# A gate moved from ScalarE to VectorE, and more gathered tiles for the ScalarE and SyncE queues, in a recommender's forward pass

## The chip, the cores and the metric

The kernel runs on one core of one Trainium2 chip. A core has five engines with a queue of instructions each: TensorE (PE, matrix products into PSUM), VectorE (DVE), ScalarE (ACT), GpSimd (POOL) and SyncE (SP). ACT, POOL and SP can also issue DMAs. The metric is the device time of one execution in microseconds, the median of three runs.

## The reference, cut to what matters

16384 users each have 69 ids (`batch_user`) and one label id. The table `emb` has 100001 rows of 96 floats.

```python
u = emb[batch_user]                       # 16384 x 69 x 96
ql = emb[batch_label[:, 0]]
q = jnp.broadcast_to(ql[:, None, :], u.shape)
z = jnp.concatenate([q, u, q - u, q * u], axis=-1)
h = _dice(z @ W1 + b1, a1, EPS_DICE)      # 64 sums for each id
h = h @ W2 + b2
att = h @ W3 + b3
eff = (batch_user < ITEM_NUM)[..., None]
pre = jnp.where(eff, u * att, 0.0)
pooled = jnp.einsum('gf,bfe->bge', window, pre).reshape(u.shape[0], G * E)
x = jnp.concatenate([pooled, ql], axis=-1)
# two layers with _dice (200 and 80 wide) and a last product give one number for each user

def _dice(x, alpha, eps):
    p = jax.nn.sigmoid(_bn_eval(x, eps))
    return (alpha * (1.0 - p) + p) * x
```

The gate of `_dice` is the factor `alpha * (1 - p) + p`, that is `(1 - alpha) * p + alpha`.

## The kernel before, in words

The users are cut into 32 blocks of 512. The ids of a block are cut into 69 chunks of 512 rows of the table: 64 main chunks (8 users times their first 64 fields) and 5 tail chunks (one of the last five fields for all 512 users). A step takes two chunks, so there are 1104 steps (`NPAIR`). A chunk has four tiles of 128 rows, so a step reads eight tiles of 128 rows of 96 floats.

How a tile gets into SBUF is the first thing to follow. Normally `gather` (line 265) issues one indirect DMA on POOL, which reads 128 ids and brings 128 rows into the step's buffer `u` (14 buffers in `upool`). Some chunks, called singles, have their fourth tile (`SLOT = 3`) brought in another way: row by row, as 128 DMAs of 384 bytes, from SP (109 tiles, the odd chunk of one step in ten, `SP_CHUNKS`) or from ACT (136 tiles, the even chunk of one step in eight, `ACT_CHUNKS`). These rows land in a buffer of `ring` (4 buffers for SP, 3 for ACT). The class `Singles` does this: `load` (line 283) reads 32 row offsets from SBUF into registers of the queue, and `fetch` (line 295) issues one DMA for each row at line 301. A single's gather on POOL is left out, and PE waits on a semaphore for its rows.

The order of all work is written out by hand: `plan` maps each step to its pieces, and every engine runs its own instructions in that order. In step i of the body this is: every fourth step the attention sums of four steps (`attend_rows`, ACT copies them out of PSUM at line 416); the tail's part; every fourth step their spreading (`spread`); the hidden sums of step i-2 (`hidden`); ACT's row DMAs of the step (`scalar_rows`); the pooling products of step i-7 (`pool`, `POOL_LAG`); and `fetch(i)`, which gathers, transposes on PE into `ptr` (two PSUM buffers), copies to `uT` and multiplies to `quT` on DVE. SP's tile for step m is put at step m-6, and SP's loads of ids (`load_ids`, line 151, four blocks each) 50 steps ahead of their block; SP runs on its own as soon as its ring has room. ACT's rows are 16 a step, eight steps to a tile, issued right after the gate of the same step, and they end three steps ahead of their use. A block's label rows (`head_gather`, four gathers on POOL) and its top layers (`top1` to `top3`) are spread over steps of their own; the last eight steps and what follows them are listed one by one, with the last block's top cut in quarters.

The other thing to follow is the gate. `hidden` (line 389) adds up the hidden sums of two chunks in PSUM (`ph`, two buffers). ACT then makes y = sigmoid(ph) at line 405 and y = (1 - a1) * y + a1 at line 406 (an Identity activation with a scale and a bias for each partition), and DVE multiplies y = ph * y at line 407. PE reads y in `attend_rows`, `attend_tail`.

Of the kernel before, what the change touches and what calls it, by code (L numbers as in the profile page):

```python
# [14 lines left out]
AF = mybir.ActivationFunctionType  # L15
ALU = mybir.AluOpType
PSUM = bass.MemoryType.PSUM

P = 128
# [29 lines left out]

ROW_BYTES = 4 * E  # L50
SLOT = 3
SP_CHUNKS = [2 * (10 * s + 8) + 1 for s in range(109)]
SP_RING = 4
ACT_CHUNKS = [2 * (8 * s + 11) for s in range(136)]
ACT_RING = 3
ACT_ROWS = 16
ACT_STEPS = -(-P // ACT_ROWS)
SINGLES = SP_CHUNKS + ACT_CHUNKS
NSB = (len(SINGLES) + P - 1) // P
NSEM = 8  # L60


def chunk_of(c):

    n, k = divmod(c, NCH)
    if n == NBLK - 1 and k >= EARLY:
        k = NMAIN + k - EARLY if k < EARLY + NTAIL else k - NTAIL
    return n, k
# [47 lines left out]
def rec_kernel(  # L116
# [12 lines left out]
    nc = tc.nc  # L129
# [1 line left out]

    const = ctx.enter_context(tc.tile_pool(name="const", bufs=1))
    ipool = ctx.enter_context(tc.tile_pool(name="ipool", bufs=2))
    upool = ctx.enter_context(tc.tile_pool(name="upool", bufs=14))
    tpool = ctx.enter_context(tc.tile_pool(name="tpool", bufs=4))
    ypool = ctx.enter_context(tc.tile_pool(name="ypool", bufs=6))
    rpool = ctx.enter_context(tc.tile_pool(name="rpool", bufs=2))
# [60 lines left out]
    a1c = NEAR.of(wn, "a1")  # L198
    na1c = const.tile([P, 1], F32, name="na1c")
# [75 lines left out]
    class Singles:  # L275

        def __init__(self, name, engine, kind, chunks, first, buffers, group):
            self.name, self.engine, self.kind, self.group = name, engine, kind, group
            self.chunks, self.first, self.buffers = chunks, first, buffers
            self.sems = [tc.alloc_semaphore(f"{name}{k}") for k in range(NSEM)]  # L280
            self.given = [0] * NSEM

# [12 lines left out]
        def fetch(self, s, start, stop):  # L295

            b, k = self.buffers[s % len(self.buffers)], s % NSEM
            for r in range(start, stop):
# [90 lines left out]
    def hidden(i, uT, quT):  # L389

        ph = ps_h.tile([P, 512], F32, tag="h", name=f"ph{i}")
        places = [chunk_of(2 * i + j) for j in range(2)]
        sums = [ph[j * H1 : (j + 1) * H1, :] for j in range(2)]
        for (n, k), p in zip(places, sums):
            if k >= NMAIN:
                nc.tensor.matmul(p, Cq, qTs[n % 2], start=True, stop=False)  # L396
        for j, ((n, k), p) in enumerate(zip(places, sums)):
            if k < NMAIN:
                nc.tensor.matmul(p, As[n % 2][:, k // 4, :], uT[j], start=True, stop=False)  # L399
            else:  # L400
                nc.tensor.matmul(p, A, uT[j][0:E], start=False, stop=False)  # L401
        for j, p in enumerate(sums):
            nc.tensor.matmul(p, Wp, quT[:, j, :], start=False, stop=True)  # L403
        y = ypool.tile([P, 512], F32, tag="y", name=f"y{i}")
        nc.scalar.activation(y, ph, AF.Sigmoid, scale=S_DICE)  # L405
        nc.scalar.activation(y, y, AF.Identity, bias=a1c, scale=na1c)  # L406
        nc.vector.tensor_mul(y, ph, y)  # L407
        return y

    def attend_rows(b, n):  # L410
# [156 lines left out]
    def hidden_of(k):  # L567
        return lambda: ys.__setitem__(k, hidden(k, *hs[k]))
# [25 lines left out]
    def at(step, *work):  # L594
        plan.setdefault(step, []).extend(work)

    by_sync = Singles("sp", nc.sync, mybir.EngineType.SP, SP_CHUNKS, 0, range(SP_RING), 32)
    for s, m in enumerate(SP_CHUNKS):
        at(max(0, m // 2 - 6), lambda s=s: by_sync.fetch(s, 0, P))

    by_scalar = Singles(
        "act",
        nc.scalar,
        mybir.EngineType.Activation,
        ACT_CHUNKS,
        len(SP_CHUNKS),
        range(SP_RING, SP_RING + ACT_RING),
        2 * ACT_ROWS,
    )
    turn = {}  # L610
    for s, m in enumerate(ACT_CHUNKS):
        for k in range(ACT_STEPS):
            turn.setdefault(m // 2 - 2 - ACT_STEPS + k, []).append((s, k * ACT_ROWS, min(P, (k + 1) * ACT_ROWS)))

    def scalar_rows(i):

        for s, start, stop in turn.get(i, []):
            by_scalar.fetch(s, start, stop)

    c = NPAIR - CLOSE  # L620
    for i in range(c):
        if i >= 3 and (i - 3) % 4 == 3:
            at(i, rows_of(i - 6, 4))
        if i >= 3:
            at(i, tails_of(i - 3))
        if i >= 4 and (i - 4) % 4 == 3:
            at(i, spread_of(i - 7, 4))
        if i >= 2:
            at(i, hidden_of(i - 2))
        at(i, lambda i=i: scalar_rows(i))  # L630
        if i < c - CLOSE:
            if i >= POOL_LAG:
                at(i, pool_of(i - POOL_LAG))
        else:

            for k in {0: (-15, -14), 1: (-13,), 3: (-12, -11), 4: (-10, -9), 7: (-8, -7)}.get(i - c + 8, ()):
                at(i, pool_of(c + k))
        at(i, fetch_of(i))
# [116 lines left out]
```

## Time and profile before

| | |
|---|---|
| median of 3 runs | 10925.68 us (10925.35 to 10929.42) |
| profiled execution | 10926.71 us, span 10924.9 us |
| PE busy | 8862.0 us, 81% |
| POOL busy | 8226.3 us, 75%, 8715 gathers |
| DVE busy | 4285.5 us, 39% |
| ACT busy | 1897.5 us, 17%, beside 17408 row DMAs |
| SP | 13952 row DMAs |
| mean granted TensorE clock | 0.745 of full speed |

In the profile an engine's share is its busy time over the span. Issuing a DMA from ACT or SP, reading registers and waiting are not counted as busy, so ACT's 17% leaves out its row DMAs; a `q` after an engine's name (ACTq, SPq) marks such instructions of its queue. A group's row has the line, engine, operation, what is written and read and how often; after the bar its busy time and the mean ns of one; after the second bar the engine's idle time just before, and what ended it. "issue" as a releaser means that the profile shows nothing the engine waited for.

### The profile page before, as it was taken

The numbers are of one execution on the slowest core, as the hardware profiler recorded it, in microseconds if no ns is written. First come the engines' busy times: TensorE is split into PE (matmuls) and PEld (weight loads), VectorE is DVE, ScalarE is ACT, GpSimd is POOL, SyncE is SP. The second block draws the span as 40 slices with busy tenths as digits, with TensorE's granted clock in tenths as the row PEclk, the third lists the DMA queues.
The fourth block names the chain that finished last, engine by engine and source line by source line (L and its number), as shares of the span: only waits on it lengthen the run. The fifth ranks groups of instructions, "written<-read, shape, count | busy, mean of one in ns | idle before, by whom it ended". The sixth has DMA issues, their size and how long they took to land.

```text
span 10924.9 us, 172203 instructions
## 1 busy us (share of the span) xinstructions
PE 8862.0 (81%) x41797; PEld 4319.5 (40%) x41797; DVE 4285.5 (39%) x7535; ACT 1897.5 (17%) x2761; POOL 8226.3 (75%) x8721
## 2 busy tenths in 40 slices
PE   7878878788887888888878778878888887888878
PEld 3333434343333344333433333334343333433335
DVE  4334333333333333433333333333333333333334
ACT  1111111111111111111111111111111111111112
POOL 7777777777777777777777777777777777777776
PEclk7767777777777777767777777777777777777777
DMA  2212211121111212212111121112212112122111
GB/s 49 42 42 44 42 42 41 42 44 42 42 42 42 44 41 42 42 41 44 42 42 41 42 44 42 42 42 42 44 42 42 42 41 44 42 42 41 42 41 36
DMA packets 344467, 458.51 MB, mean 42 GB/s; under 512 B 202354, under 2 KB 202866, under 8 KB 343330
## 3 DMA queue, kind: packets, MB, share of 16 engines
q0 software_dynamic: 278880, 428.92, 18.7%
q1 hardware_dynamic: 29762, 11.82, 0.5%
q10 hardware_dynamic: 34816, 6.75, 0.4%
q8 instruction: 336, 5.51, 0.2%
q14 instruction: 673, 5.51, 0.2%
HBM read 446.74 MB, written 0.07 MB: 41 GB/s over the span
## 4 chain that ended last, share of the span: by engine, by line
POOL 49%; issue 21%; PE 17%; DMA 12%; DVE 0%; ACT 0%; ACTq 0%; POOLq 0%; DVEq 0%
POOL u L266 48%; DMA u<-in_rows,ids 12%; PE p L502 4%; PE acc L325 4%; PE ph L399 3%; PE ph L403 2%; PE ptr L325 2%; POOL q L266 1%; PE prow L414 1%; PE pa L423 1%; PE ph L396 0%; PE ph L401 0%; PE pc L348 0%; PE patt L431 0%; ACTq L301 0%
## 5 line engine op out<-in xcount | busy, mean ns | idle before, releaser
L266 POOL DMA_INDIRECT u<-in_rows,ids x8587 | 8104.3, 944 | 2620.1 <-issue 2428.2
L325 PE MATMUL ptr<-ident,u 128*96 128x128 f32 x8587 | 2002.8, 332 | 1940.1 <-DMA u<-in_rows,ids 1892.9
L407 DVE TENSOR_TENSOR y<-ph,y 128x512 f32<-128x512 f32 x1104 | 763.5, 692 | 4377.1 <-ACT y L406 4119.6
L325 PEld LDWEIGHTS ptr<-ident,u 128*96 128x96 f32 x8587 | 1139.7, 149 | 2701.4 <-DMA u<-in_rows,ids 2262.6
L325 PEld LDWEIGHTS acc<-rw,u 128*96 128x96 f32 x15930 | 1677.0, 187 | 1204.3 <-issue 977.6
L376 DVE COPY uT<-ptr 96x512 f32<-96x512 f32 x2208 | 1494.1, 677 | 1488.6 <-PE ptr L325 1485.2
L325 PE MATMUL acc<-rw,u 128*96 128x20 f32 x15930 | 1792.5, 258 | 57.8 <-DVE rw L436 41.7
L405 ACT ACTIVATE y<-ph 128x512 f32<-128x512 f32 x1104 | 658.6, 597 | 6308.6 <-PE ph L403 5822.7
L399 PE MATMUL ph<-uT,A 128*64 128x512 f32 x4096 | 1649.8, 883 | 0.0
L403 PE MATMUL ph<-quT,wn 96*64 96x512 f32 x4416 | 1585.2, 788 | 0.0
L379 DVE TENSOR_TENSOR quT<-ptr,qT 96x512 f32<-96x512 f32 x2048 | 1380.2, 674 | 0.0
L406 ACT ACTIVATE y<-y,wn,na1c 128x512 f32<-128x512 f32 x1104 | 898.1, 813 | 36.6
L403 PEld LDWEIGHTS ph<-quT,wn 96*64 96x64 f32 x4416 | 440.7, 188 | 1041.5 <-issue 1040.8
L502 PE MATMUL p<-pooled,wf 96*100 96x512 f32 (+1 forms) x1400 | 693.1, 644 | 0.0
L399 PEld LDWEIGHTS ph<-uT,A 128*64 128x64 f32 x4096 | 264.1, 175 | 616.2 <-issue 608.8
L416 ACT COPY row<-prow 128x512 f32<-128x512 f32 (+1 forms) x277 | 161.6, 583 | 1791.9 <-PE prow L414 1179.1
L470 DVE COPY pooled<-acc 96x160 f32<-96x160 f32 x1008 | 419.9, 417 | 117.6 <-PE acc L325 116.9
L414 PE MATMUL prow<-y,v 128*32 128x512 f32 x2208 | 453.6, 891 | 1.4 <-DVE y L407 1.1
L502 PE MATMUL p<-pre,V 96*100 96x512 f32 (+1 forms) x700 | 394.9, 710 | 3.0 <-DVE x L485 2.7
L502 PEld LDWEIGHTS p<-pooled,wf 96*100 96x100 f32 x1400 | 259.5, 198 | 332.6 <-issue 332.6
L436 DVE SCALAR_TENSOR_TENSOR rw<-patt,bb,wn 128x320 f32<-128x320 f32 x554 | 276.2, 539 | 143.6 <-PE patt L431 142.9
L431 PE MATMUL patt<-ident,row 128*128 128x128 f32 x1108 | 224.9, 340 | 25.1 <-DVE pre L424 22.7
(72 smaller groups left out, 2445.8 us busy)
## 6 DMA issues: line engine op xcount, KB each, us to landing
ring<-in_rows ACTq DMA_DIRECT2D x17408, 0.4 KB
ring<-in_rows SPq DMA_DIRECT2D x13952, 0.4 KB
u<-in_rows,ids POOLq DMA_INDIRECT x8587
ids<-in_idx SPq DMA_DIRECT2D x8, 560.0 KB, 3.9
q<-in_emb,ids POOLq DMA_INDIRECT x128
wf<-in_far SPq DMA_DIRECT2D x1, 1209.0 KB, 6.4
wn<-in_near SPq DMA_DIRECT2D x1, 236.0 KB, 2.8
ids<-in_idx SPq DMA_DIRECT2D x1, 140.0 KB, 2.3
```

The lines of the kernel that those rows point to most:

```text
L266: nc.gpsimd.indirect_dma_start(out=dst, out_offset=None, in_=table, in_offset=bass.IndirectOffsetOnAxis(ap=index, axis=0),)
L325: ins = op(out, ring[:, at[0]].bitcast(F32) if at else u[:, 4 * (c % 2) + t, :], other, **how)
L376: nc.vector.tensor_copy(uT[j][0:E], ptr)
L379: nc.vector.tensor_tensor(quT[:, j, :].rearrange("e (s f) -> e s f", f=FM), ptr.rearrange("e (s f) -> e s f", f=FM), by_field(q[:, k * NS ...
L399: nc.tensor.matmul(p, As[n % 2][:, k // 4, :], uT[j], start=True, stop=False)
L403: nc.tensor.matmul(p, Wp, quT[:, j, :], start=False, stop=True)
L405: nc.scalar.activation(y, ph, AF.Sigmoid, scale=S_DICE)
L406: nc.scalar.activation(y, y, AF.Identity, bias=a1c, scale=na1c)
L407: nc.vector.tensor_mul(y, ph, y)
L414: nc.tensor.matmul(pr[32 * k : 32 * (k + 1), :], v2, ys[b + k], start=True, stop=True)
L470: nc.vector.tensor_copy(pooled[n][:, :, k * NS : (k + 2) * NS].rearrange("e g s -> e s g"), pa.rearrange("e j s g -> e (j s) g"),)
L502: nc.tensor.matmul(p1, w[:, h * DH : (h + 1) * DH], x, start=(k == 0), stop=(k == KTOP - 1))
```

## The change

The gate's second operation leaves ACT. With s the sigmoid, DVE makes y = (s * (1 - a1)) * ph and then y = ph * a1 + y, two scalar_tensor_tensor operations in place of one product. ACT is left with the sigmoid. More tiles become singles: SP has 199, one every 5.5 steps, with a ring of 8 buffers; ACT has 187, with a ring of 4, and its rows are one stream of 22 a step, in order, whatever tile they belong to, ending two steps ahead of the tile's use. `u` has a fifteenth buffer. The space in SBUF for the descriptors of POOL's DMAs, 16384 bytes of each partition by default, is set to 4096.

```diff
-SP_CHUNKS = [2 * (10 * s + 8) + 1 for s in range(109)]
-SP_RING = 4
-ACT_CHUNKS = [2 * (8 * s + 11) for s in range(136)]
-ACT_RING = 3
-ACT_ROWS = 16
-ACT_STEPS = -(-P // ACT_ROWS)
+SP_CHUNKS = [2 * (int(5.5 * s) + 6) + 1 for s in range(199)]
+SP_RING = 8
+ACT_ROWS = 22
+ACT_CHUNKS = [2 * ((s + 1) * P // ACT_ROWS + 2) for s in range(187)]
+ACT_RING = 4
...
+RING_BYTES = 4096
...
-    upool = ctx.enter_context(tc.tile_pool(name="upool", bufs=14))
+    upool = ctx.enter_context(tc.tile_pool(name="upool", bufs=15))
...
         nc.scalar.activation(y, ph, AF.Sigmoid, scale=S_DICE)
-        nc.scalar.activation(y, y, AF.Identity, bias=a1c, scale=na1c)
-        nc.vector.tensor_mul(y, ph, y)
+        nc.vector.scalar_tensor_tensor(y, y, na1c, ph, ALU.mult, ALU.mult)
+        nc.vector.scalar_tensor_tensor(y, ph, a1c, y, ALU.mult, ALU.add)
...
-        2 * ACT_ROWS,
+        32,
...
-    turn = {}
-    for s, m in enumerate(ACT_CHUNKS):
-        for k in range(ACT_STEPS):
-            turn.setdefault(m // 2 - 2 - ACT_STEPS + k, []).append((s, k * ACT_ROWS, min(P, (k + 1) * ACT_ROWS)))
-
     def scalar_rows(i):
 
-        for s, start, stop in turn.get(i, []):
-            by_scalar.fetch(s, start, stop)
+        row, stop = i * ACT_ROWS, min((i + 1) * ACT_ROWS, len(ACT_CHUNKS) * P)
+        while row < stop:
+            s, start = divmod(row, P)
+            n = min(P - start, stop - row)
+            by_scalar.fetch(s, start, start + n)
+            row += n
...
-    nc = bacc.Bacc("TRN2", target_bir_lowering=False, num_devices=1)
+    nc = bacc.Bacc("TRN2", target_bir_lowering=False, num_devices=1, dynamic_dma_scratch_size=RING_BYTES)
```

## The prediction

> **What bounds the kernel now.** I read the page first, then the instructions on the tiles `u` and `ring`, then the waits, then short timelines.
>
> ```profile
> span 10924.9 us, 172203 instructions
> ...
> PE 8862.0 (81%) x41797; PEld 4319.5 (40%) x41797; DVE 4285.5 (39%) x7535; ACT 1897.5 (17%) x2761; POOL 8226.3 (75%) x8721
> ...
> L266 POOL DMA_INDIRECT u<-in_rows,ids x8587 | 8104.3, 944 | 2620.1 <-issue 2428.2
> L325 PE MATMUL ptr<-ident,u 128*96 128x128 f32 x8587 | 2002.8, 332 | 1940.1 <-DMA u<-in_rows,ids 1892.9
> ```
>
> By busy share PE looks like the limit. But POOL's idle time is "issue": it waits for nothing the profile shows, 0.30 us after each 0.944 us gather, while PE's idle time before its transposes (ptr) is a wait for those gathers. The chain of work says the same: POOL 49%, issue 21%, DMA 12%, PE 17%.
>
> ```profile
> L266 POOL DMA_INDIRECT u<-in_rows,ids x8587: 940/944/1092, 8.8 to 10886.8; - x200
> ```
>
> ```profile
> L266 POOL DMA_INDIRECT q<-in_emb,ids x128: 940/944/1334, 3.3 to 10418.6; - x128
> ```
>
> 8587 + 128 = 8715 gathers start from 3.3 to 10886.8 us: 10883.5/8714 = 1.249 us each, with no gap over 0.3 us (waits). POOL is a metronome from start to end; 3.3 us lie before it and 10924.9 - 10886.8 = 38.1 us after its last start. So time is the number of gathers x 1.249 us plus about 41 us, as long as everybody else keeps up.
>
> The others' room: transposes start on average 5.3 us after their gather's start (trace, paired one by one), at most 26 us, and with 14 buffers of u, each freed seven steps later, POOL would stall only at some 60 us. The two row streams (shortest, median and longest ns of an instruction):
>
> ```profile
> L301 ACTq DMA_DIRECT2D ring<-in_rows x17408: 213/213/530, 18.4 to 10748.1; - x198
> L301 SPq DMA_DIRECT2D ring<-in_rows x13952: 227/228/463, 6.3 to 10459.8; - x200
> ```
>
> The offset loads that go with them, and SP's own waits:
>
> ```profile
> L286 ACTq TENSOR_LOAD <-offsets x544: 2132/2182/2236, 16.1 to 10735.1; - x182
> L286 SPq TENSOR_LOAD <-offsets x436: 2027/2174/2411, 4.1 to 10447.1; - x146
> ```
>
> ```profile
> SPq L301 <- PE ptr L325: 3556.9, 71, 95.2
> SPq L301 <- PE acc L325: 1324.8, 26, 96.8
> ```
>
> SP waits 4882 us for free ring buffers: it is idle nearly half the time. On ACT a row of 384 bytes, its register move included, costs what the spacing in a timeline shows:
>
> ```profile
> 5000.03 9.90 SPq L301 DMA_DIRECT2D ring<-in_rows  x31
> ```
>
> ```profile
> 5007.62 0.81 ACT L406 ACTIVATE y<-y,wn,na1c 128x512 f32<-128x512 f32 x1
> 5007.68 4.77 ACTq L301 DMA_DIRECT2D ring<-in_rows  x16
> ```
>
> (9.90 - 0.23)/30 = 0.322 us per row on SP, (4.77 - 0.21)/15 = 0.304 on ACT; over all adjacent starts under 0.6 us apart the means are 0.3255 and 0.320, and ACT's is 0.326 while SP also issues. ACT's sequencer goes on to the rows as soon as the Identity has started.
>
> [...] ACT's 213 ns become 223 to 241 ns beside SP's stream. [...] The trace shows the first reader 2.4 us after a gather's start, so two or three gathers are in flight.
>
> **The change part by part.**
>
> 1. Singles: 109 + 136 = 245 tiles become 199 + 187 = 386. POOL loses 141 gathers of 8715: 141 x 1.249 = -176.1 us. The step falls from 8715 x 1.249/1104 = 9.86 us to 8574 x 1.249/1104 = 9.70.
>
> 2. SP: 199 tiles, each 128 x 0.3255 + 4 offset loads of 2.18 (2.25 with the moves around them) = 41.7 + 9.0 = 50.7 us, against 5.5 steps x 9.70 = 53.4 us. Hidden with 5% to spare; the ring of 8 lets it run tiles ahead (a buffer is asked for 44 steps after its predecessor was due, and released after 7 to 8). The ids loads queued behind SP's rows (0.4 us of issue each) are planned 50 steps early. If the cover goes, tile after tile comes late and PE waits.
>
> 3. ACT: per step it was 16 rows, half an offset load, sigmoid and Identity: about 16 x 0.32 + 0.5 x 2.25 + 0.63 (the Identity waits for the sigmoid) = 6.9 us. It becomes 22 x 0.326 = 7.17, 22/32 loads x 2.25 = 1.55, and about 0.3 for dispatch and for row copies and the top's activations ahead of a sigmoid: 9.0 us of 9.70. Hidden, but only by 7%. Queued behind those rows is the next sigmoid, so a late ph (PE to ACT) now meets a queue busy for up to 9.7 us (a step with a load) instead of 8.1. Waiting for it: y on DVE, behind it the copies pooled and uT/quT, and then PE's next acc and ptr. PE has most of a step before it needs them, ACT's own least cycle stays under POOL's step, and PE's own step is 8862/1104 = 8.03 us, so lags come and are made up. Cost on the path in the body: 0.
>
> 4. DVE: the product (0.692 us) becomes two scalar_tensor_tensor on 128x512. Nearest rows: the pre STT, 0.741 us, and the x STT on 100x512, 0.751, both PSUM with SBUF. 1104 x (2 x 0.75 - 0.69) = 894 us more, 5180 us or 48% of the span: hidden under POOL's cadence. Bounds 0.69 and 0.85 each give 760 and 1115 us, both hidden. ACT loses 1104 x 0.813 = 898 us. Sigmoid to y stays about 2.1 us (0.60 + 0.81 + 0.69 before, 0.60 + 2 x 0.75 after).
>
> 5. POOL's descriptor space, 16384 by default to 4096 bytes: no row shows its price. Gathers 1024 apart (568, 1592, 2616 and so on) take 961 instead of 944 ns[...]; four times as often is 34 x 17 ns = 0.6 us. From below: nothing says a smaller ring makes POOL faster. From above: if each gather had to ask for space, the price is unknown; 176.1/8574 = 20.5 ns per gather would eat the gain. I take 0.
>
> 6. The fifteenth buffer of u is one more step of room: 0. Doubled offsets (128 x 512 integers): two DVE operations of 0.29 us become about 0.6 at the start, beside POOL: 0.
>
> 7. The end is where PE nearly sets the pace, as these windows of 200, 200 and 87 us show:
>
> ```profile
> 10400.00:10600.00 200.00, 155.45 (x778) 78.69 (x780) 79.01 (x138) 34.27 (x50) 151.18 (x161) 0.71 0.20 41
> 10600.00:10800.00 200.00, 168.96 (x798) 90.10 (x795) 75.43 (x135) 37.22 (x56) 151.20 (x161) 0.79 0.19 41
> 10800.00:10887.00 87.00, 78.60 (x451) 50.77 (x449) 39.53 (x72) 18.53 (x30) 65.67 (x71) 0.76 0.19 40
> ```
>
> PE is busy 155.45/200 = 78% in the first, 84% in the second and 90% in the last. Its lag behind POOL climbs to 25 us near 10650, falls to 5 by 10730, climbs to 25 near 10760 and is 4 to 7 at the last gather. With ACT at 9.0 us a step PE can no longer run the first recovery at 7 to 8 us a step (ACT's rows last to step 1088), and two more singles lie in the last 24 steps, 2.5 us less of POOL. I estimate +8 us at the end, between 0 and 20.
>
> Sum against the profiled execution, 10926.71 us: -176.1 + 8 = 10758.6. It stands 1.0 us over the median of the three runs, 10925.68; so 10758 us, -1.5%.
>
> **The rivals.**
>
> A, partial: ACT and PE don't overlap ideally at 93% load. In steps where PE itself takes 10 to 11.6 us (the qT and A rows, the top's matmuls) ACT starves, and afterwards it makes up 0.7 us a step at most. For: that small margin, and the jitter of ph (5 to 14 us between successive sums, nine times in ten). Against: taking the longer of PE's own time and 9.0 us step by step gives 9.2 to 9.3 us, still under 9.70. If it averages 9.8: +0.1 x 1088 = +109 us, 10,867.
>
> B, slower: ACT's sequencer becomes the bound. One stream tied to the sigmoids can't run ahead. Its threshold is 9.70 us a step to begin to show, (10926 - 45 - 157)/1088 = 9.86 us to lose everything (157 us: the last 16 steps). At a row cost of 0.37 us beside a busier SP: 8.14 + 1.55 + 0.3 = 10.0, hence 1088 x 10.0 + 157 + 45 = 11,080 us.[...] Against: ACT's 7555 adjacent rows beside SP already average 0.326.
>
> C, the small descriptor space stalls POOL: at +30 ns a gather, 10758 + 257 = 11,015.[...]
>
> D, SP falls behind: over 53.4 us a tile it bounds; at 55, 199 x 55 + 9 x 9.9 + 45 = 11,080. Against: 50.7, and ACT beside it moves SP's row only from 0.325 to 0.326.
>
> **How the numbers follow.** Forecast 0.76 (10,748 to 10,780); A 0.13 (10,780 to 10,904); B 0.06, C 0.03 and D 0.02 mostly slower. A measurement of this kernel can tell about 0.2%, 22 us, from no change. Most of A is faster, its edge the same; B, C and D give slower 0.10. Faster 0.87, same 0.03, slower 0.10. The floor is 8574 x 1.249 + 41 = 10,750, less a little for the unsure end: low 10,745. High 10,840 takes in the nearer half of A and leaves out under 2 in 10.
>
> **What would show it.** POOL: 8446 gathers of u at 1.249 us, idle only "issue". PE still waits for u, less than 1893 us. ACT's idle time before the sigmoid shrinks, with waits on "issue" larger than 117 us. SP's waits for the ring fall from 4882 to about 500 us. Two STT groups of 0.75 us. Wrong if POOL shows waits over 0.3 us, if a gather's period has changed, if PE's waits move from u to ring (late rows) or to DVE, or if the tail after POOL's last gather exceeds 60 us.

## The result, and the profile after

| | before | after |
|---|---|---|
| median | 10926.22 us (10924.22 to 10931.77) | 10939.76 us (10930.91 to 10947.42) |
| profiled execution, its span | 10926.71, 10924.9 us | 10932.42, 10930.6 us |
| gathers on POOL | 8715 | 8574 |
| mean of start to start | 1.249 us | 1.270 us |
| after POOL's last gather has started | 38.1 us | 43.1 us |

The ratio is 1.0012, with an interval of 95% from 1.0005 to 1.0019: the kernel is not 168 us faster, as forecast, but slower by 0.12%, which is less than the 0.2% that the prediction held to be the least that can be told from no change. These are the lines of the page of the kernel after that answer to those shown of before, with its queues and the shares of its chain.

```profile
span 10930.6 us, 207736 instructions
...
PE 8797.1 (80%) x41797; PEld 4332.6 (40%) x41797; DVE 5119.1 (47%) x8639; ACT 985.9 (9%) x1657; POOL 8093.3 (74%) x8580
...
q0 software_dynamic: 274368, 421.98, 20.3%
q1 hardware_dynamic: 52802, 16.42, 2.6%
q10 hardware_dynamic: 47872, 9.29, 2.1%
...
POOL 31%; DMA 29%; issue 15%; PE 14%; ACTq 9%; DVE 1%; ACT 1%; POOLq 0%
...
L266 POOL DMA_INDIRECT u<-in_rows,ids x8446 | 7971.7, 944 | 2752.6 <-issue 2321.2
L325 PE MATMUL ptr<-ident,u 128*96 128x128 f32 x8446 | 1893.5, 331 | 1604.8 <-DMA u<-in_rows,ids 1536.7
L406 DVE SCALAR_TENSOR_TENSOR y<-y,na1c,ph 128x512 f32<-128x512 f32 x1104 | 824.5, 747 | 4201.6 <-ACT y L405 4137.7
...
L407 DVE SCALAR_TENSOR_TENSOR y<-ph,wn,y 128x512 f32<-128x512 f32 x1104 | 829.3, 751 | 39.0
```

The 141 gathers are gone and a gather still takes 944 ns. But POOL's idle time before a gather has risen from 2620.1 us for 8587 (0.305 us each) to 2752.6 us for 8446 (0.326 us each). From start to start a gather takes 0.0206 us more (1.2696 for 1.2490): 0.0206 us x 8573 intervals = 177 us, and the gathers saved were worth 176.1 us. With 5.0 us more after the last gather, that accounts for the profiled execution: 10924.9 - 176.1 + 177 + 5.0 = 10930.8 against a span of 10930.6 us. In the chain, DMA has gone from 12% to 29%.

Which wait it is, the waits of POOL say (idle us in total, times, longest). Before:

```profile
POOL u L266 <- issue: 2428.2, 7958, 0.3
...
POOL u L266 <- DMA u<-in_rows,ids: 111.1, 364, 0.3
```

After:

```profile
POOL u L266 <- issue: 2321.2, 7552, 1.5
...
POOL u L266 <- DMA u<-in_rows,ids: 314.1, 632, 2.5
```

Before, no wait is longer than 0.3 us whatever it is put down to, so these are only labels on the ordinary pause between two gathers. After, POOL waits up to 2.5 us, and the releaser is a DMA that writes `u`: an earlier gather of its own. A timeline of POOL in a bad stretch shows one such knot (start, duration, and in brackets the idle time just before and its releaser):

```profile
3750.46 0.94 POOL L266 DMA_INDIRECT u<-in_rows,ids  x1 [0.30 <-issue]
3752.01 0.94 POOL L266 DMA_INDIRECT u<-in_rows,ids  x1 [0.61 <-DMA u<-in_rows,ids]
3753.82 0.94 POOL L266 DMA_INDIRECT u<-in_rows,ids  x1 [0.87 <-DMA u<-in_rows,ids]
3755.69 0.94 POOL L266 DMA_INDIRECT u<-in_rows,ids  x1 [0.92 <-DMA u<-in_rows,ids]
```

Which gather it waits for is in the trace's semaphore events. In this program a gather adds 1 to its semaphore sixteen times (all sixteen stand in the trace for 8044 of the 8574 gathers after, some are missing for the others), and the semaphores of the gathers are eight, 122 to 129, in rotation. A gather starts once the one eight back has all its sixteen: of 8036 such pairs none starts less than 0.258 us after the sixteenth. For the gather at 3753.82 us, the one eight back had started 10.85 us earlier; fifteen of its increments had come by 2.42 us after its start, the sixteenth at 10.59 us. POOL went on 0.26 us later. Over all gathers whose sixteen increments are in the trace:

```
from a gather's start, us                 before    after
15th increment, median                      2.46     2.49
16th increment, median                      2.52     7.60
16th increment, 95% of gathers are below    3.63    10.14
a row DMA, from its issue to its last byte, median   0.9    4.3 to 4.4
a row's data packet, median ns              22       173 to 175
```

Fifteen sixteenths of each gather land as fast as before. One sixteenth is late, and so are the rows. Eight gathers at 1.249 us are 9.99 us; less the 0.26 us, a sixteenth that lands more than some 9.7 us after its gather's start should stop POOL (an estimate), and that is the upper end of the distribution after. Of the 8036 pairs, 386 have a gather that starts over 0.1 us late, and in 322 of these the sixteenth had taken more than 9.7 us.

What the one late share has in common with the rows is, in my reading, their place: one of the sixteen DMA engines that the page counts. The packets speak for it. A row DMA has one data packet of 384 bytes and one packet of 4 bytes, by size and number its increment (ACT's queue q10 holds 2 x 17408 packets before and 2 x 23936 after), where a gather has sixteen data packets of 3072 bytes and sixteen of 4 (q0: 32 x 8715 = 278880 before). The trace doesn't number its DMA engines, so that all rows lie on the same one isn't seen; that exactly one share of sixteen is late fits it. The queues' shares say how much the rows' part is. Of before:

```profile
q0 software_dynamic: 278880, 428.92, 18.7%
q1 hardware_dynamic: 29762, 11.82, 0.5%
q10 hardware_dynamic: 34816, 6.75, 0.4%
```

The last column is a share of sixteen engines. 0.9% for the two rows' queues (q1 SP, q10 ACT) would be at most 14% of one engine, if all rows lie there (SP's queue also carries the ids and weights, 0.2%); after, 2.6 + 2.1 = 4.7% would be at most 75% of one, on top of that engine's part of the gathers, some 20% if their sixteen shares are alike. Packets' times overlap (those of the two queues add up to 8198 us after and cover 6472), so this is a sign and not an occupancy: the rows have grown by a factor of 1.58 (49408 for 31360), the two queues' time by 5.

The stalls are not spread evenly. Windows of the kernel after (busy us and number of instructions of PE, PEld, DVE, ACT and POOL, then clock, DMA share and GB/s):

```profile
1000.00:2000.00 1000.00, 799.50 (x3712) 389.66 (x3714) 460.43 (x773) 88.04 (x147) 726.96 (x771) 0.74 0.26 42
2000.00:3000.00 1000.00, 805.83 (x3763) 386.88 (x3755) 459.81 (x768) 88.71 (x148) 723.56 (x767) 0.74 0.26 41
4500.00:5500.00 1000.00, 799.15 (x3842) 394.06 (x3838) 467.80 (x788) 89.84 (x151) 747.78 (x793) 0.75 0.26 43
6000.00:7000.00 1000.00, 807.67 (x3871) 401.23 (x3872) 473.44 (x797) 89.79 (x152) 751.34 (x797) 0.75 0.26 43
```

The same window before:

```profile
2000.00:3000.00 1000.00, 805.04 (x3841) 387.99 (x3839) 388.21 (x682) 174.97 (x254) 755.66 (x801) 0.75 0.20 42
```

POOL starts 767 gathers in the third thousand microseconds against 801 before, later 793 to 797. Up to about 3800 us SP runs ahead: it has waited for free buffers of the ring 2.5 us in all until 3500 us, and issues 2.50 rows per us, which is all it can (128 rows in 50.7 us are 2.52). ACT adds 2.17, together 4.67 rows per us with 0.770 gathers. Then SP's eight buffers are full, its rate falls to 2.38, and together the two make 4.64 rows per us with 0.795 gathers. The sixteenth increment has its median at 9.0 us in the first stretch (1000 to 3500 us) and at 6.9 us in the second (4000 to 10000 us). Before, it was 1.28 + 1.62 = 2.9 rows per us.

### The profile page after: what moved, and what is told of

The parts are those of the page before. It is cut to its first block, busy times and chain, and to the rows that moved or that the text cites. A ratio compares the mean times of both kernels' runs of the same rounds, so it can differ in the third digit from the quotient of the medians.

```text
span 10930.6 us, 207736 instructions
## 1 busy us (share of the span) xinstructions
PE 8797.1 (80%) x41797; PEld 4332.6 (40%) x41797; DVE 5119.1 (47%) x8639; ACT 985.9 (9%) x1657; POOL 8093.3 (74%) x8580
## 4 chain that ended last, share of the span: by engine, by line
POOL 31%; DMA 29%; issue 15%; PE 14%; ACTq 9%; DVE 1%; ACT 1%; POOLq 0%
POOL u L266 31%; DMA u<-in_rows,ids 28%; ACTq L301 7%; PE p L502 3%; PE acc L325 2%; ACTq L286 2%; PE ph L403 2%; PE ph L399 2%; PE ptr L325 2%; PE prow L414 1%; PE pa L423 1%; PE ph L396 0%; PE ph L401 0%; POOL q L266 0%; DMA q<-in_emb,ids 0%
## 5 line engine op out<-in xcount | busy, mean ns | idle before, releaser
L266 POOL DMA_INDIRECT u<-in_rows,ids x8446 | 7971.7, 944 | 2752.6 <-issue 2321.2
L325 PE MATMUL ptr<-ident,u 128*96 128x128 f32 x8446 | 1893.5, 331 | 1604.8 <-DMA u<-in_rows,ids 1536.7
L406 DVE SCALAR_TENSOR_TENSOR y<-y,na1c,ph 128x512 f32<-128x512 f32 x1104 | 824.5, 747 | 4201.6 <-ACT y L405 4137.7
L399 PE MATMUL ph<-uT,A 128*64 128x512 f32 x4096 | 1606.4, 860 | 0.0
L403 PE MATMUL ph<-quT,wn 96*64 96x512 f32 x4416 | 1553.4, 773 | 0.0
L407 DVE SCALAR_TENSOR_TENSOR y<-ph,wn,y 128x512 f32<-128x512 f32 x1104 | 829.3, 751 | 39.0
L502 PE MATMUL p<-pooled,wf 96*100 96x512 f32 (+1 forms) x1400 | 634.7, 598 | 0.0
L414 PE MATMUL prow<-y,v 128*32 128x512 f32 x2208 | 528.0, 884 | 90.2 <-DVE y L407 85.1
L502 PE MATMUL p<-pre,V 96*100 96x512 f32 (+1 forms) x700 | 427.8, 761 | 23.6 <-DVE x L485 23.3
L485 DVE SCALAR_TENSOR_TENSOR x<-p,wf,g 100x512 f32<-100x512 f32 (+3 forms) x105 | 73.9, 704 | 508.6 <-ACT g L484 508.6
```

What stands on the lines that cost most here:

```text
L266: nc.gpsimd.indirect_dma_start(out=dst, out_offset=None, in_=table, in_offset=bass.IndirectOffsetOnAxis(ap=index, axis=0),)
L325: ins = op(out, ring[:, at[0]].bitcast(F32) if at else u[:, 4 * (c % 2) + t, :], other, **how)
L406: nc.vector.scalar_tensor_tensor(y, y, na1c, ph, ALU.mult, ALU.mult)
L407: nc.vector.scalar_tensor_tensor(y, ph, a1c, y, ALU.mult, ALU.add)
L414: nc.tensor.matmul(pr[32 * k : 32 * (k + 1), :], v2, ys[b + k], start=True, stop=True)
L502: nc.tensor.matmul(p1, w[:, h * DH : (h + 1) * DH], x, start=(k == 0), stop=(k == KTOP - 1))
```

## The experiments

**Theory** (E in the texts below). All rows queue at one DMA engine. Up to some rate they cost a gather nothing; near that engine's limit the gather's share there waits behind rows, and past eight gathers of delay POOL stalls. It must vanish with fewer rows, whichever queue they leave from, and shrink if SP can't run ahead. **Rivals** after the result: the smaller descriptor space slows POOL (R; rival C of the prediction); the gate's second operation holds up DVE's other work, and with it PE, or disturbs POOL (G); ACT's queue with its 22 rows a step sets the pace (S); SP's stream alone, or ACT's alone, is at fault. And, within the theory, two readings of "limit": so many bytes, or so many DMAs.

**The two edits that had been priced at nothing, each alone on the kernel before.** First the descriptor space:

```diff
-num_devices=1)
+num_devices=1, dynamic_dma_scratch_size=4096)
```

> The kernel before with POOL's descriptor space cut from 16384 to 4096 bytes, and nothing else. Theory E (the row DMAs of SP and ACT fill one of the 16 DMA engines, so that engine's share of each gather lands late and POOL waits for the gather eight back): no change, 10,926 us within 10, last share of a gather landing 2.5 us after its start. Rival R (the small descriptor space delays the gathers or stalls POOL): slower, 10,926 + about 176 us = 11,100, since in the changed kernel the stalls add up to 172 us over nearly as many gathers.

Measured: 10927.34 us beside 10927.04 of the kernel before, ratio 1.0000 (0.9991 to 1.0009). The sixteenth increment comes at 2.53 us. Then the gate:

```diff
-nc.scalar.activation(y, y, AF.Identity, bias=a1c, scale=na1c)
-nc.vector.tensor_mul(y, ph, y)
+nc.vector.scalar_tensor_tensor(y, y, na1c, ph, ALU.mult, ALU.mult)
+nc.vector.scalar_tensor_tensor(y, ph, a1c, y, ALU.mult, ALU.add)
```

> The kernel before with the gate on VectorE alone (two scalar_tensor_tensor for the Identity and the product), rows and rings as before. Theories E, R and S (ScalarE's 22 rows a step, at about 9 us of its queue, set the pace): no change, 10,926 us within 10. Rival G (the two longer operations on VectorE hold up uT and pooled, and with them PE): slower, 10,935 or more.

Measured: 10928.14 us, ratio 1.0000 (0.9991 to 1.0009), sixteenth increment at 2.53 us. Rivals R and G are out; both costs of nothing were right.

**SP's singles back to 109, all else as in the kernel after.**

```diff
-SP_CHUNKS = [2 * (int(5.5 * s) + 6) + 1 for s in range(199)]
-SP_RING = 8
+SP_CHUNKS = [2 * (10 * s + 8) + 1 for s in range(109)]
+SP_RING = 4
```

> The changed kernel with SP's old tiles, 109 at one in ten steps with a ring of 4; ScalarE keeps its 22 rows a step and 187 tiles, the descriptor space stays at 4096. 296 singles leave 8960 - 296 = 8664 gathers. Theory E: SP's half load frees the DMA engine, POOL runs at 1.249 us again: 8664 x 1.249 + 41 = 10,862 us, to 10,875 with some loss at the end; last landing back at 2.5 to 4 us. Rivals S and R: ScalarE's queue and the descriptor space are as they were, so still 10,930 to 10,945.

Measured: 10863.14 us beside 10927.04, ratio 0.9941 (0.9924 to 0.9958). With 296 singles 8664 gathers are left, and 8664 x 1.249 + 41 = 10,862. The waits of POOL in this kernel:

```profile
POOL u L266 <- issue: 2422.3, 7938, 0.3
POOL u L266 <- DMA u<-in_rows,ids: 89.1, 292, 0.3
```

Nothing is longer than 0.3 us again, at 3.52 rows per us. ACT's stream of 22 rows a step is therefore not the fault by itself, and S is out; every gather saved pays.

**Only SP's ring back from 8 to 4 buffers.** All rows and all 8574 gathers stay.

```diff
-SP_RING = 8
+SP_RING = 4
```

> The changed kernel with SP's ring cut from 8 to 4 buffers; the same 386 singles and the same instructions otherwise. Theory E: SP can run ahead by about 1.6 tiles instead of 5.6, so its stretch at full speed (2.50 rows per us, up to 3800 us in the changed kernel, gathers 1.30 us apart) ends after some 1000 us; then 2.38 rows per us and 1.257 us per gather. That saves (1.30 - 1.257) x about 2200 gathers = 95 us: 10,845 us, between 10,815 and 10,870. Rivals S and R: no change, 10,940; a rival of late rows (SP has too little lead) would make it slower, over 10,950.

Measured: 10859.06 us (10842.96 to 10870.47), ratio 0.9941 (0.9924 to 0.9957). Its windows:

```profile
1000.00:2000.00 1000.00, 805.45 (x3815) 397.40 (x3816) 467.96 (x788) 90.15 (x152) 743.16 (x789) 0.75 0.26 42
2000.00:3000.00 1000.00, 810.32 (x3888) 393.31 (x3890) 473.23 (x797) 91.49 (x153) 751.40 (x797) 0.76 0.27 43
```

The stretch in which SP runs ahead ends by about 1000 us instead of 3800, and the window from 2000 to 3000 us has 797 gathers in place of 767. That fits the ring's size: four buffers are 512 rows, and SP gains on its readers by 2.50 less 128/(5.5 x 10.1) = 2.30 rows per us, so they last some 2600 us. (10.1 us is the step while POOL stalls.) Somewhat under half of the lost gain (81 of 182 us) was thus the buffers that I had counted as SP's safety. The rest stays: in the profiled execution, the fastest of the four, the median of the sixteenth is still 7.1 us, and the stalls add up to 82 us.

**ACT's singles back to 136, SP's left at 199.** The other queue, to see whether it matters whose rows go.

```diff
-ACT_ROWS = 22
-ACT_CHUNKS = [2 * ((s + 1) * P // ACT_ROWS + 2) for s in range(187)]
+ACT_ROWS = 16
+ACT_CHUNKS = [2 * ((s + 1) * P // ACT_ROWS + 2) for s in range(136)]
```

> The changed kernel with ScalarE back at 16 rows a step and 136 tiles; SP keeps 199 tiles and its ring of 8. 335 singles leave 8960 - 335 = 8625 gathers. Theory E: SP at full speed with ACT gives 2.50 + 1.62 = 4.1 rows per us, under the 4.65 at which the engine was full, so no stall even while SP runs ahead: 8625 x 1.249 + 41 = 10,814 us, to 10,825. A rival in which SP's running ahead is harmful whatever ACT does[...]: still stalls early, 10,880 or more.

Measured: 10816.19 us beside 10927.62, ratio 0.9899 (0.9879 to 0.9919); 8625 x 1.249 + 41 = 10,814. Its rows' queues:

```profile
q1 hardware_dynamic: 52802, 16.36, 0.8%
q10 hardware_dynamic: 34816, 6.75, 0.5%
```

SP's queue carries exactly the packets that it carries in the kernel after, and their share is 0.8% where it was 2.6%. POOL has no wait for a gather over 0.3 us, at 4.12 rows per us:

```profile
POOL u L266 <- DMA u<-in_rows,ids: 99.2, 325, 0.3
```

So SP's stream isn't the fault by itself either; the sum is.

**Spreading a row over the engines.** Two kernels wrote the row as 16 or as 2 pieces, in the hope that each piece would go to another engine:

```diff
-out=ring[r : r + 1, b], in_=row_bytes[:, bass.ds(self.values[r], ROW_BYTES)]
+out=ring[r : r + 1, b].rearrange("p (k n) -> p k n", k=16),
+in_=row_bytes[:, bass.ds(self.values[r], ROW_BYTES)].rearrange("p (k n) -> p k n", k=16),
```

> The changed kernel with each row DMA written as 16 pieces of 24 bytes instead of one of 384[...]. Theory E says that today the rows lie on one engine: then the gap between the 15th and the 16th share of a gather's landing (2.5 and 7.6 us) closes. If an engine's time for a row goes with its bytes, POOL returns to 1.249 us and the time to about 10,755; if each piece costs an engine nearly what the row costs, all 16 fill up and all shares land late: 10,940 or more. The issue spacing on SP and ACT may also grow with 16 pieces: over 0.35 us a row SP's tile of 5.5 steps no longer fits and the time goes over 10,940 for that reason, which the row spacing would show. Against E: a lone 16th share still landing near 7.6 us.

> The same with two pieces of 192 bytes for each row. Theory E with cost by bytes: one engine's load of rows halves, two shares of each gather land somewhat late (2.5 to 4 us) and the time is about 10,755. With cost by piece: both engines are as full as one was, two shares land at 7 to 8 us, and the time stays at 10,940.

Measured: 10942.23 and 10947.20 us, one time each. The trace shows the same single packet of 384 bytes for each row as before: pieces that follow each other in memory had been put together again. These are two repetitions of the kernel after, and say nothing of spreading. So the pieces were set apart, in a second copy of the table with gaps between a row's pieces (an input prepared with it), two of 192 bytes or sixteen of 24:

```diff
-in_=row_bytes[:, bass.ds(self.values[r], ROW_BYTES)]
+in_=row_bytes[:, bass.ds(self.values[r], 416)].rearrange("p (k n) -> p k n", k=2)[:, :, 0:192]
```

> The changed kernel, but the rows of the singles are read from a second copy of the table in which each row lies as two halves of 192 bytes, 16 bytes apart, so that a row's DMA keeps two pieces (in the two runs meant for this before, the pieces were merged back into one of 384 bytes). Theory E, rows on one engine: the pieces go to two engines. With an engine's time going by bytes its load of rows halves: the 15th and 16th share of a gather land at 2.5 to 4 us, POOL returns to 1.25 us, 10,755 to 10,800. With time by piece: two engines are as full as one was, the 15th and 16th share both land near 7.5 us, and the time stays at 10,940. Against E: only the 16th is late, as before. If the queues take over 0.35 us to issue a row of two pieces, SP falls behind and the time is over 10,940 for that reason.

> The same with 16 pieces of 24 bytes, 8 bytes apart (512 bytes a row). By bytes: every engine gets a sixteenth of the rows' load, all shares land at 2.5 to 3 us, POOL at 1.249 us, 10,750 to 10,765. By piece: all 16 shares land late, 7 us or more, 10,940 or more. Queues slower than 0.35 us a row: SP late, over 10,940, with PE waiting for ring.

Measured: 21013.61 us with two pieces (ratio 1.923, 1.917 to 1.929) and 18513.91 us with sixteen (1.694, 1.689 to 1.699). SP's instructions for the rows in the first of the two (shortest, median, longest ns):

```profile
L302 SPq DMA_DIRECT2D ring<-in_apart x25472: 2/616/1547, 6.9 to 20893.4; - x199
```

Issuing such a row takes SP 616 ns in place of 228, rows start 0.73 us apart (median), and the chain of this kernel is SP's own queue:

```profile
SPq 83%; issue 14%; ACTq 1%; PE 1%; DMA 0%; DVE 0%; ACT 0%; POOL 0%; POOLq 0%
```

The pieces did stay apart: a row has two data packets of 192 bytes and two of 4 in the one kernel, sixteen of 24 and sixteen of 4 in the other (q10: 4 x 23936 = 95744 packets and 32 x 23936 = 765952). Whether the pieces went to as many engines was not shown. The sixteenth increment is back at 2.48 us, but at 2.4 rows per us that says nothing: it is 2.52 us at the 2.90 of before. Both kernels are failures as tests of the engine. Whether rows can be spread without paying for it in the issue stays open.

**By bytes or by number.** Each row DMA moves only the first 96 of its 384 bytes; three quarters of each single's row are left out of the computation.

```diff
-out=ring[r : r + 1, b], in_=row_bytes[:, bass.ds(self.values[r], ROW_BYTES)]
+out=ring[r : r + 1, b, 0:96], in_=row_bytes[:, bass.ds(self.values[r], 96)]
```

It ran beside a version with SP's tiles 5.75 steps apart (below). There the kernel before itself took 13766.58 us where its median was 10,926 to 10,928 everywhere else, so nothing is read from this pair, and both were run again.

> The changed kernel with each row DMA moving only the first 96 of the 384 bytes; the other three quarters of a single's row stay zero, so this part of the gather is left out. Number of row DMAs, issue and waits as in the changed kernel. Theory E with an engine's time going by bytes: the load of rows falls to a quarter, the 16th share of a gather lands at 2.5 to 3 us and POOL runs at 1.249 us: 8574 x 1.249 + 41 = 10,750, to 10,765. With time going by the number of rows: nothing changes, 10,940, the 16th share at 7.6 us. In between, by both. A rival that lays the loss to anything else than what the rows move (ScalarE's queue, the gate, SP's lead): 10,940.

> Between the best run so far (SP every 6 steps, 369 singles, 10,792 us) and the changed tiles with a ring of 4 (SP every 5.5 steps, 386 singles, 10,859): SP every 5.75 steps, 190 tiles, ring of 4; 377 singles leave 8583 gathers, floor 8583 x 1.249 + 41 = 10,761. Theory E: 128/(5.75 x 9.72) + 22/9.72 = 4.55 rows per us, just under the 4.65 at which the engine was full, and SP gains only 5.2 us a tile while it fills its ring, so stalls for some 1100 us: 10,785 to 10,825. If the limit is a matter of singles and not of rates: between 10,792 and 10,859 in proportion, 10,825.

These gave 16743.60 and 16437.67 us. Again:

> The changed kernel with each row DMA moving only the first 96 of the 384 bytes (three quarters of a single's row are left out), once more, on a chip where the kernel before takes its usual 10,926 us; the first time that kernel took 13,767 us beside it. With an engine's time going by bytes: the 16th share of a gather lands at 2.5 to 3 us, POOL at 1.249 us, 10,750 to 10,765. By the number of rows: nothing changes, 10,940, 16th share at 7.6 us. A rival that lays the loss to anything else than what the rows move: 10,940.

Measured: 10923.55 us (10918.31 to 10935.37) beside 10927.60, ratio 0.9998 (0.9988 to 1.0007). The queues:

```profile
q1 hardware_dynamic: 52802, 9.09, 3.3%
q10 hardware_dynamic: 47872, 2.39, 3.2%
```

A quarter of the rows' bytes, and the packets' times add up to more, not less: 6.5% of sixteen engines would be 104% of one. Here too the times overlap (laid over each other, those of the two queues cover 5857 us of 10927). The sixteenth increment comes at 7.31 us (7.60 with whole rows). POOL's idle time before gathers is in this line of the page:

```profile
L267 POOL DMA_INDIRECT u<-in_rows,ids x8446 | 7993.7, 946 | 2723.5 <-issue 2334.1
```

It is 147 us over the 8446 x 0.305 of an undisturbed POOL (177 with whole rows). So five sixths of the stalls are still there with a quarter of the bytes. By itself this run can't tell a limit by number from a loss that has nothing to do with what the rows move; the runs with fewer rows rule the latter out. Together they say that between 96 and 384 bytes what counts is mainly the number of DMAs.

**Fewer rows, to find where the limit lies.** SP with 182 tiles, one every six steps, and four buffers, ACT as in the kernel after:

```diff
-SP_CHUNKS = [2 * (int(5.5 * s) + 6) + 1 for s in range(199)]
-SP_RING = 8
+SP_CHUNKS = [2 * (6 * s + 6) + 1 for s in range(182)]
+SP_RING = 4
```

> Meant to beat both: the changed kernel with SP at one tile in 6 steps (182 tiles) and a ring of 4. 369 singles leave 8591 gathers: floor 8591 x 1.249 + 41 = 10,771 us. Theory E: rows at 128/(6 x 9.72) + 22/9.72 = 4.46 per us in the steady part, below 4.65, so stalls only in the first 800 us while SP fills its ring: 10,775 to 10,795. If the engine is already full at 4.46, or ScalarE's queue costs something of its own: over 10,810.

Measured: 10792.06 us (10785.50 to 10792.36) beside 10927.62, ratio 0.9875 (0.9858 to 0.9891). Then 190 tiles, 5.75 steps apart:

```diff
+SP_CHUNKS = [2 * (int(5.75 * s) + 6) + 1 for s in range(190)]
+SP_RING = 4
```

> SP every 5.75 steps, 190 tiles, ring of 4, once more, for the same reason; 377 singles leave 8583 gathers, floor 8583 x 1.249 + 41 = 10,761. Theory E: 4.55 rows per us in the steady part, just under the 4.65 at which the engine was full: 10,785 to 10,825. If the loss goes with the number of singles alone: in proportion between 369 and 386, 10,825.

Measured: 10786.15 us (10783.33 to 10787.03) beside 10927.60, ratio 0.9871 (0.9854 to 0.9887). This is faster than both kernels, by 1.3% and 1.4%. Its page and its waits:

```profile
q1 hardware_dynamic: 50498, 15.91, 2.1%
q10 hardware_dynamic: 47872, 9.29, 1.7%
...
L266 POOL DMA_INDIRECT u<-in_rows,ids x8455 | 7981.6, 944 | 2596.6 <-issue 2402.3
```

```profile
POOL u L266 <- issue: 2402.3, 7866, 0.7
...
POOL u L266 <- DMA u<-in_rows,ids: 110.3, 331, 2.4
```

POOL's idle time is 2596.6/8455 = 0.307 us a gather, next to the 0.305 of before; stalls are 17 us, nearly all of them in the first 1000 us. 8583 x 1.249 + 41 = 10,761; the stalls and a tail of 43.8 us in place of 38.1 make most of the rest. The two versions, with 8591 and 8583 gathers, can't be told apart by their times. All kernels that carried whole rows and weren't bound by SP's queue, in order of their rate in steady running:

```
                              rows per us   16th increment   stalls of POOL   time
before                           2.90           2.52 us           2 us        10926.22
SP 109, ACT 187                  3.52           2.64              2           10863.14
SP 199, ACT 136                  4.12           2.79              2           10816.19
SP 182, ACT 187                  4.46           3.97              8.5         10792.06
SP 190, ACT 187                  4.55           4.97             17           10786.15
SP 199, ACT 187, ring of 4       4.64           7.11             82           10859.06
SP 199, ACT 187 (after)      4.67, 4.64         7.60            172           10939.76
```

Stalls are start to start beyond 1.249 us, where it is over 0.1 us, in the profiled execution; 2 us of them are some longer gathers in the first 130 us, in every kernel. The rates differ by up to 2% between stretches of one run. The delay is nearly flat to 4.1 rows per us, doubles by 4.55 and runs away at 4.64. With 0.8 gathers per us, that is where gathers begin to give way. It fits the two stretches of the kernel after as well: where SP pushes more rows in, fewer gathers pass (4.67 with 0.770, 4.64 with 0.795). That the losses come to just the 176 us of the gain is a coincidence of these rates, as the ring of four buffers shows.

## Why the prediction was wrong

The forecast of 10758 us and its range from 10,745 to 10,840 both missed; no change within 0.2% had been given 3 in 100. By its own steps:

1. **Singles, -176.1 us.** The count and the 944 ns were right. The error is in the factor 1.249: the view showed POOL as a metronome, and the sum took its period for a property of POOL. It is one only while the gather eight back has landed in time. Where fewer rows go beside them, the gathers left out pay in full: 51 of them with SP's 109 tiles (10863 us, 10,862 by the same formula), 90 with ACT's 136 (10816 and 10,814).
2. **SP, 50.7 of 53.4 us.** Right in its rate (2.50 rows per us seen, 2.52 worked out), wrong in its reading. "Hidden with 5% to spare; the ring of 8 lets it run tiles ahead" counted the lead as safety; it put more rows beside the gathers for 3800 us (4.67 per us, and 0.770 gathers), and taking half of the ring away gave 80 us back. SP's waits for the ring fell from 4882 to 319 us, 500 predicted:

```profile
SPq L301 <- PE ptr L325: 253.9, 76, 16.0
SPq L301 <- PE acc L325: 63.6, 11, 14.5
```

3. **ACT, 9.0 of 9.70 us.** Right: a sigmoid starts 1.9 us after its sums on average (0.35 before), half of the sigmoids still wait for PE, and PE runs 11.1 us behind the gathers on average, at most 31. Of the signs named, ACT's waits on "issue" before a sigmoid grew, from 117 to 1177 us, but its idle time there grew too (6309 to 6727 us) instead of shrinking. Rivals A and B, which had most of the doubt, didn't occur: with SP's tiles back at 109 and the same 22 rows a step on ACT, the time is that of the gathers at 1.249 us again.
4. **DVE, two operations at 0.75 us.** 0.747 and 0.751, hidden: the gate alone leaves the time as it was.
5. **Descriptor space, nothing.** Right in its result, and rival C is refuted. But the argument was beside the point: it looked for the limit in the descriptors, and POOL waited for the one of eight semaphores that came round again (the knot above: 10.59 us, with 9.99 for eight gathers). The smaller space can be seen, and at the size worked out: every 256th gather (312, 568, 824 and so on) now takes about 960 ns, where every 1024th did. And "two or three gathers are in flight" was read from before, where a gather lands after 2.5 us; that number was part of what the change moved.
6. **Fifteenth buffer and offsets, nothing.** No run set them apart. PE's lag of at most 31 us never came near the 60 at which buffers would count.
7. **The end, +8 us.** +5.0.

The step that failed lies between parts 1, 2 and 3: I priced 18,048 more row DMAs by what they cost SP and ACT to issue, and by nothing at all on the DMA engines that carry them. The page of before gave no warning by its height: 0.9% of sixteen engines for the rows, 20% in all. It was the division that was missing: a row has one data packet, so if all rows lie on one engine (my inference, not shown) they are up to 14% of it and not 0.9% of sixteen. Even so, 14% times 1.58 would have forecast no limit; what before couldn't show is the bend at 4.5 rows per us. An honest sum would have taken that cost as unknown, with the whole gain as its upper bound, and a fifth rival: a late share of the gathers, deciding once it lands later than 9.7 us.

The signs named in advance found it: "wrong if POOL shows waits over 0.3 us, if a gather's period has changed".

## What to carry to other kernels

Price a DMA three times: where it is issued, on the DMA engines that carry it, and by what waits for its neighbours there. A row here has a single data packet where a gather has sixteen, and one sixteenth of each gather came late beside the rows (7.60 us, the others by 2.49). So take the share of such transfers times sixteen as an upper bound: here 75% of one engine (an estimate from the queues' 4.7%), which the mean DMA share of 0.26 hides. A constant period of an engine is a fact of its present surroundings, so ask which semaphore ends it and how late that semaphore could come (here: the gather eight back, 2.5 us of 9.7 used). Deeper buffers for a producer that is not the bound let it run ahead, and here the one that is was slower while it did (4.67 rows per us with 0.770 gathers, then 4.64 with 0.795).

## What the runs showed of the hardware

- One sixteenth of a gather can be late by itself: fifteen increments at 2.49 us, the sixteenth at 7.60. A mean DMA share of 0.26 goes with it.
- Row DMAs of one partition from SP and ACT pass at about 4.6 per us beside 0.8 gathers per us; at 4.67 the gathers fell to 0.770, and no run asked for more. At 96 bytes each the stalls stay five sixths as large. What sets this number wasn't found, nor did a run raise the eight gathers in flight.
- A row whose source has gaps is dear to issue: 616 ns on SP in two pieces and 541 ns in sixteen, against 228 ns in one; pieces that adjoin came out as one packet of 384 bytes, in 10942.23 and 10947.20 us beside 10939.76 with one piece.
- A quarter of the descriptor space for POOL (4096 for 16384 bytes) doesn't change the time: ratio 1.0000 (0.9991 to 1.0009). In the kernel after, every 256th gather takes about 960 ns in place of every 1024th.
